# Delta rule: inverses of two successive pairs stated side by side, their transfers queued behind those stated last, and k times q a step behind q's convolution

## The chip, the core and the metric

The kernel runs on one core of a Trainium2 chip. The metric is the time of one execution on the device, in microseconds. A core has five engines that work at the same time, each through its own instructions in a fixed order: TensorE (PE in the profile; its weight loads are PEld), VectorE (DVE), ScalarE (ACT), GpSimd (POOL) and SyncE (SP). SP computes nothing here: it sends the transfers (DMAs) between device memory and on-chip memory, one after the other, and an instruction that waits for a semaphore holds up those behind it in its queue.

## What is computed

The program is one decoder layer in float32 on x of shape 4 x 512 x 512: a gated delta rule over 16 heads of 128, a cross attention, a self attention and a mixture of 8 experts. The change lies in the first part. Its reference, cut:

```
q = _causal_conv(x @ Wq.T, cw_q, cb_q)      # 4 taps, then silu; k and v the same
...
g = jnp.exp(-jnp.exp(A_log)[None, None, :] * jax.nn.softplus(a + dt_bias[None, None, :]))
beta = jax.nn.sigmoid(b)
q = _l2norm(q.reshape(Bb, Ss, H, DK))
k = _l2norm(k.reshape(Bb, Ss, H, DK))
...
def step(Sstate, inputs):
    q_t, k_t, v_t, g_t, beta_t = inputs
    retrieved = jnp.einsum('bhkv,bhk->bhv', Sstate, k_t)
    error = v_t - g_t[..., None] * retrieved
    update = k_t[..., :, None] * (beta_t[..., None] * error)[..., None, :]
    Snew = g_t[..., None, None] * Sstate + update
    o_t = jnp.einsum('bhkv,bhk->bhv', Snew, q_t)
    return (Snew, o_t)
...
o = o * jax.lax.rsqrt(jnp.mean(o * o, axis=-1, keepdims=True) + EPS) * norm_w
o = o * jax.nn.silu(x @ Wg.T)
return o @ Wo.T
```

## The kernel before

The 512 steps of the scan are taken in 4 chunks of 128. Within a chunk the steps become a linear system with a triangular matrix of 128 x 128, and its inverse makes them into matrix products. The work goes by **pairs**: pair m is two of the 16 heads of one sequence, 32 pairs in all (4 sequences of 8 pairs). A pair has four parts:

- stage1(m), lines 530 to 632: k's products (line 511), convolution (519, 522, 525), its turning round (554), its squared length ss (559, 565) and from it, on POOL, rk, ee, ke and nr (566 to 570; nr is appended to `factors`); the decays em (a scan on VectorE, 575, over the row that line 538 loads); the triangular matrices at (587), which go to device memory (588); then `load_blocks`, which loads their 32 diagonal blocks of 32 x 32, one a partition, as iA (642), and a table of identities as iT (641). After that q's convolution, qg = q times a row of decays (598, POOL; the row comes by another transfer of line 538), the product of k and q with its decays, pt (607, 609), and q's squared length, which goes through sr (616, 618) and a transfer (622) into rq, and is raised to a power on POOL (630, 631).
- stage2_inverse(m), lines 645 to 668: 31 elimination steps on the 32 blocks at once, each two instructions (654, 655) that depend on each other, on VectorE for even m and on POOL for odd m. Then the inverses and their transposes (659) go to device memory (658 into t_d, 660 into x_d) and come back as 128 x 128 tiles T (663) and X (665).
- stage2_values(m), lines 682 to 705: v's and the gate's products and convolutions (511 to 525), v turned round and scaled (694, 696); line 687 sends rq on its way to a row.
- stage3(m), lines 712 to 829: T and X are completed out of their 32-blocks (lines 726 to 760: four groups of small products, each waiting for a copy on ScalarE), rrow is loaded (764), and then come the chunks one after the other: r (778, 780), u (787, 789), the next state (797, 800 or 802) and the outputs (805, 807). At its end lines 819, 823, 827 and 828 scale the output and sum its squares. output(m), line 833, multiplies by Wo (852, 857).

The main loop (952 to 985) runs over m. In round m it takes the 15 steps of stage3(m), and after each of them one step of `rest`: `turns` gives every generator in it its number of steps, that is one of output(m-1), two of stage1(m+2), one of stage2_values(m+1) and two of inversions(m, ...). What is left of `rest` is stated after stage 3. This order of statement isn't yet the order in which the engines work: the layer below (a scheduler) orders each engine's instructions, by its own idea of what is ready when, and it keeps data dependences and the edges that `tc.issue_after(ins)` gives: whatever is stated inside that block for the engine of `ins` comes behind `ins` on that engine. The main loop so queues the rest behind the last of stage 3's vector instructions (`vital`), and the odd pairs' elimination steps behind the latest nr (`factors`). SP's transfers have no such edge.

`inversions` states the inverse of pair m+1 to its end, and only then, from step 10 of stage 3 on and if the blocks have been asked for, begins that of pair m+2, which is carried on in the next round (`begun`). `inverses` holds the blocks of a pair before its inverse, and T and X after it.

Weights are loaded ahead by line 502, the rows of decays by line 538, each into one buffer: the load waits until the last reader of what it overwrites is done. T has one buffer, X two.

Of the kernel before, what the change touches and what calls it, by code (L numbers as in the profile page):

```python
# [31 lines left out]
F32 = mybir.dt.float32  # L32
# [6 lines left out]
P = 128  # L39
B, S, D = 4, 512, 512  # L40
NT = B * S // P
TB = S // P
# [3 lines left out]
HG = 2  # L46
# [52 lines left out]
def decoder(ctx: ExitStack, tc: tile.TileContext, a: dict, out: bass.AP):  # L99
    nc = tc.nc  # L100
# [38 lines left out]
    def chain(*gs):  # L139
        for g in gs:  # L140
            yield from g
# [31 lines left out]
    def run(*gs):  # L173
        for g in gs:
            for _ in g:
                pass

    def turns(*gs):

        gs = [(g, n) for g, n in gs if g is not None]  # L180
        while gs:
            left = []
            for g, n in gs:
                if all(next(g, gs) is not gs for _ in range(n)):
                    left.append((g, n))
            gs = left
            yield
# [138 lines left out]
    with ExitStack() as st:  # L326
# [3 lines left out]
        w2 = st.enter_context(tc.tile_pool(name="a_2", bufs=2))  # L330
# [32 lines left out]
        inv_d = [[dram.tile([HG * TB, CH], F32, name=f"{k}_d{n}") for k in "tx"] for n in range(2)]  # L363
# [18 lines left out]
        def squares(d):  # L382

            return d[:, : P * P].rearrange("c (r t) -> r c t", r=P)

        def blocks(d):

            f = d.rearrange("c x -> (c x)").rearrange("(n x) -> n x", x=BLK)
            return f[:, : 32 * P].rearrange("n (r t) -> n r t", r=32)[:, :, 0:32]
# [4 lines left out]
        def scale(dst, src, by, p):  # L394

            for c in range(TB):
                nc.scalar.activation(dst[:, c, :], src[:, c, :], AF.Identity, scale=by[:, p * TB + c : p * TB + c + 1])

        seqs = {}

        def prologue(b):
# [128 lines left out]
        def stage1(m):  # L530
# [12 lines left out]
            for p in range(HG):  # L543
                t = live.tile([P, S], F32, name="kT")
# [6 lines left out]
            for p in range(HG):  # L551
# [3 lines left out]
                t = s1.tile([P, TB, P], F32, name="ktok")  # L555
# [22 lines left out]
            ats = []  # L578
# [15 lines left out]
            for p in range(HG):  # L594
                q = s1.tile([P, S], F32, name="qh")
                yield from conv(b, hg, p, 0, wq, q)
                g = live.tile([P, S], F32, name="qg", bufs=6)
                nc.gpsimd.tensor_tensor(g, q, mb[p], ALU.mult)
                qg.append(g)
                t = w2.tile([P, S], F32, name="cv", bufs=5)  # L600
                nc.scalar.activation(t, q, AF.Square)
                sq.append(t)
                yield
                pq = p_b.tile([P, TB, P], F32, name="pb")
                for c in range(TB):
                    cs = slice(c * P, (c + 1) * P)
                    nc.tensor.matmul(pq[:, c, :], kT[p][:, cs], q[:, cs], start=True, stop=True)
                t = live.tile([P, TB, P], F32, name="pt", bufs=6)
                nc.vector.tensor_tensor(t, pq, em[p], ALU.mult)
                pt.append(t)  # L610
                yield
# [13 lines left out]
            for p in range(HG):  # L625
                t = live.tile([P, TB, P], F32, name="kdec", bufs=4)
# [5 lines left out]
            keys[m] = (kT, kd_, qg, pt, nr, rq)  # L632


        inverses, begun, vital, factors = {}, {}, [], []

        def load_blocks(m, ats):

# [6 lines left out]
        def stage2_inverse(m):  # L645

            nb = HG * TB * 4
            A, T, W, ats = inverses.pop(m)
            eng = nc.vector if m % 2 == 0 else nc.gpsimd
            for i in range(31):  # L650
                n, w = 31 - i, i + 1
                u = W[:, : n * w].rearrange("p (a b) -> p a b", a=n)
                with tc.issue_after(factors[-1]) if m % 2 else ExitStack():
                    eng.tensor_tensor(u, A[:, i, i + 1 :].unsqueeze(2).to_broadcast([nb, n, w]), T[:, i, :w].unsqueeze(1).to_broadcast([nb, n, w]), ALU.mult)  # L654
                    eng.tensor_tensor(T[:, i + 1 :, :w], T[:, i + 1 :, :w], u, ALU.add)  # L655
                yield
            dT, dX = inv_d[m % 2]
            nc.sync.dma_start(blocks(dT), T)
            eng.tensor_copy(A, T.rearrange("p t j -> p j t"))
            nc.sync.dma_start(blocks(dX), A)  # L660
            yield
            t = w2.tile([P, HG * TB, P], F32, name="T", bufs=1)
            nc.sync.dma_start(t, squares(dT))
            x = w2.tile([P, HG * TB, P], F32, name="X", bufs=2)
            nc.sync.dma_start(x, squares(dX))
            Ts, Xs = ([v[:, p * TB : (p + 1) * TB, :] for p in range(HG)] for v in (t, x))
            inverses[m] = (Ts, Xs, ats)
            yield

        def inversions(m, step, turn):  # L670

            if m + 1 < NP:
                yield from begun.pop(m + 1) if m + 1 in begun else stage2_inverse(m + 1)
            if m + 2 < NP:
                while turn and (turn[0] < step or m + 2 not in inverses):
                    yield
                begun[m + 2] = stage2_inverse(m + 2)
                while turn:
                    next(begun[m + 2])
                    yield  # L680

        def stage2_values(m):

            b, hg = divmod(m, NHG)
            nr, rq = keys[m][4:]
            wv, wg = weights.pop((m, 2)), weights.pop((m, 3))
            nc.sync.dma_start(r_d[m % SLOTS].rearrange("c t -> (c t)").rearrange("(n k) -> n k", k=HG * TB), rq)
            v_, gs = [], []
            for p in range(HG):
                t = yield from conv(b, hg, p, 2, wv, None)  # L690
                yield
                tp = p_b.tile([P, TB, P], F32, name="pb")
                for c in range(TB):
                    nc.tensor.transpose(tp[:, c, :], t[:, c * P : (c + 1) * P], ident)
                v = w2.tile([P, TB, P], F32, name="vn", bufs=4)
                nc.vector.tensor_tensor(v, tp, along(nr[:, p * TB : (p + 1) * TB], P), ALU.mult)
                v_.append(v)
                yield
            load_weights(m + 1, 2)
            for p in range(HG):  # L700
                g = w2.tile([P, S], F32, name="gs", bufs=3)
                yield from conv(b, hg, p, 3, wg, g)
                gs.append(g)
            load_weights(m + 1, 3)
            pairs[m] = (v_, gs)
# [6 lines left out]
        def stage3(m):  # L712
# [1 line left out]
            b, hg = divmod(m, NHG)  # L714
            xnT, beta, gam, ngam, gend, gall = seqs[b]
            kT, kd_, qg, pt, _, _ = keys.pop(m)
            Ts, Xs, ats = inverses.pop(m)
            v_, gs = pairs.pop(m)

            half = [slice(p * 64, (p + 1) * 64) for p in range(HG)]  # L720
# [228 lines left out]

        run(itertools.islice(pair0, 3 * HG + 1))  # L950
        run(turns((stage2_inverse(0), 2), (chain(pair0, turns((stage1(1), 2), (stage2_values(0), 1))), 1), (prepare(), 1)))
        for m in range(NP):
            rest, turn = [], [0]
            if m == NP - 2:
                first.close()
                x_keep = top.enter_context(tc.tile_pool(name="x_keep", bufs=1, side="right", reuse_waits="tile"))
                wq, wpj = (x_keep.tile([P, KD, D], F32, name=n) for n in ("wq", "wpj"))
                nc.sync.dma_start(wq, a["b_wq"].rearrange("(k p) c -> p k c", p=P))
                nc.sync.dma_start(wpj, a["b_wp"].rearrange("(k p) c -> p k c", p=P))
                bq, bp = rows(x_keep, "bq", "b_bq", D), rows(x_keep, "bp", "b_bp", D)  # L960
                x_kT, x_val = x_keep.tile([P, KD, M], F32, name="x_kT"), x_keep.tile([P, 2, D], F32, name="x_val")
                nc.sync.dma_start(x_kT, x_kT_d)
                nc.sync.dma_start(x_val, x_val_d)
            if m == NP - 1:
                second.close()
                wx = top.enter_context(tc.tile_pool(name="b_x", bufs=2, side="right", reuse_waits="tile"))
                rest.append((cross(0), 2))
            if m:
                rest.append((chain(idle(1), output(m - 1)), 1))
            if m + 2 < NP:  # L970
                if (m + 2) % NHG == 0:
                    assert (m + 2) // NHG in seqs
                rest.append((stage1(m + 2), 2))
            if m + 1 < NP:
                rest.append((stage2_values(m + 1), 1))
                rest.append((inversions(m, 10, turn), 2))
            if (m + 4) % NHG == 0 and (m + 4) // NHG < B:
                rest.append((prologue((m + 4) // NHG), 1))
            rest = turns(*rest)
            for _ in stage3(m):  # L980
                with tc.issue_after(vital[-1]) if vital else ExitStack():
                    next(rest, None)
                turn[0] += 1
            turn.clear()
            run(rest)
        run(turns((output(NP - 1), 1), (cross(1), 2)))
# [573 lines left out]
```

## Time and profile before

| what | us |
|---|---|
| three runs | 4069.01, 4071.47, 4080.96 |
| median | 4071.47 |
| the profiled execution | 4070.2 |
| its span, from first to last instruction | 4068.4 |
| first product of stage 3 of pair 0 | 150.3 |
| the same of pair 31 | 2310.8 |

From 150 to 2311 us the core works on the delta rule, and after that on the parts that the change doesn't touch. Between the first products of stage 3 of two successive pairs lie 66 to 76 us: mostly some 67 where the later pair is odd, some 73 where it is even.

The views used are: the page (busy time and shares of each engine), the list of waits (who waited for whom: us in total, times, longest us), the timeline of one engine (start, duration, engine, line, operation, what it writes and reads, and in brackets the idle time before it and what ended it), and the windows (busy time, granted clock, share of the DMA engines and GB/s in a stretch). SPq is SP's queue; a transfer's line there tells when it was sent, not when it landed. A line of matmuls counts two records for each float32 product.

### The profile page before, as it was taken

The page shows a single profiled execution, that of the slowest core. Times are in us where ns is not written, and L with a number is a line of the kernel's source. Part 1 is how long each engine was busy: PE and PEld are TensorE (multiplying, and loading weights), DVE is VectorE, ACT ScalarE, POOL GpSimd, SP SyncE. Part 2 cuts the span into 40 slices and gives each one's busy share as a digit, 9 for nine tenths or more (in the row PEclk, how much of TensorE's full clock was granted, in tenths as well). Part 3 has the DMA queues.
Part 4 walks back from the last instruction along what each step waited for, and adds up shares of the span by engine and source line. Part 5 has one row for each costly group of instructions (what it writes and reads, how often), then busy time and mean ns, then how long its engine had stood idle before and what let it go on. Part 6 is the DMA issues. An engine that isn't in the chain of part 4 may idle for free. (4 is left out here: it accounts for less than half of the span.)

```text
span 4068.4 us, 48733 instructions
## 1 busy us (share of the span) xinstructions
PE 3452.6 (85%) x16466; PEld 1942.1 (48%) x16466; DVE 2273.2 (56%) x4923; ACT 1572.8 (39%) x4379; POOL 1390.2 (34%) x1941
## 2 busy tenths in 40 slices
PE   5878787877978787887878788999999999899797
PEld 3545444444544444444444444555555555555343
DVE  5556656565755656665565545555665666555211
ACT  2434443333534343443334324444444444444121
POOL 1435434443543444354344522121211211211342
PEclk8989998898989898998989878999999999999898
DMA  5332333323333322323232334544444544456344
GB/s 152 88 103 90 103 90 103 94 74 103 101 98 86 113 82 85 107 87 118 85 102 68 96 118 134 163 148 145 149 140 139 162 141 143 130 170 221 74 83 92
DMA packets 391880, 465.56 MB, mean 114 GB/s; under 512 B 128451, under 2 KB 242115, under 8 KB 391440
## 3 DMA queue, kind: packets, MB, share of 16 engines
q1 hardware_dynamic: 380080, 438.03, 35.2%
q0 software_dynamic: 10112, 21.58, 2.9%
q10 hardware_dynamic: 1440, 2.84, 0.2%
q8 instruction: 132, 2.16, 0.2%
q14 instruction: 116, 0.95, 0.1%
HBM read 401.76 MB, written 64.81 MB: 115 GB/s over the span
## 5 line engine op out<-in xcount | busy, mean ns | idle before, releaser
L511 PE MATMUL pb<-xnT,w 128*128 128x512 f32 x2048 | 1027.7, 641 | 0.0
L522 DVE SCALAR_TENSOR_TENSOR cv<-pb,pp,cv 128x509 f32<-128x509 f32 (+2 forms) x576 | 423.3, 742 | 481.7 <-ACT cv L519 475.0
L511 PEld LDWEIGHTS pb<-xnT,w 128*128 128x128 f32 x2048 | 398.5, 207 | 423.8 <-issue 397.5
L1102 PE MATMUL pb<-c_q,hT 128*128 128x512 f32 x768 | 360.9, 609 | 6.3 <-DMA c_q<-in_c_wq_dram 3.7
L654 POOL TENSOR_TENSOR iW<-iA,iT 32x31 f32<-32x31 f32 (+15 forms) x496 | 259.3, 523 | 154.6 <-issue 69.5
L655 POOL TENSOR_TENSOR iT<-iT,iW 32x31 f32<-32x31 f32 (+15 forms) x496 | 285.8, 576 | 38.9
L726 PE MATMUL pb<-T,at 128*32 128x32 f32 x512 | 19.8, 236 | 325.2 <-DMA T<-t_d 325.2
L566 POOL TENSOR_TENSOR rk<-ss,mhalf 128x8 f32<-128x8 f32 x32 | 52.7, 1648 | 665.7 <-DVE ss L565 665.7
L519 ACT ACTIVATE cv<-pb,pp 128x512 f32<-128x512 f32 x192 | 148.7, 775 | 321.3 <-PE pb L511 321.1
L852 PE MATMUL pb<-wot,og 128*128 128x512 f32 x512 | 250.2, 611 | 4.7 <-DVE cv L522 4.7
L1208 PE MATMUL pw<-c_o,oT 128*128 128x512 f32 x512 | 241.3, 602 | 2.9 <-DVE oT L1200 2.9
L655 DVE TENSOR_TENSOR iT<-iT,iW 32x31 f32<-32x31 f32 (+15 forms) x496 | 229.9, 464 | 11.5
L1102 PEld LDWEIGHTS pb<-c_q,hT 128*128 128x128 f32 x768 | 144.0, 196 | 163.3 <-issue 152.6
L654 DVE TENSOR_TENSOR iW<-iA,iT 32x31 f32<-32x31 f32 (+15 forms) x496 | 215.2, 434 | 9.2
L1174 ACT ACTIVATE e<-pb,nm,rq 128x128 f32<-128x128 f32 (+3 forms) x256 | 157.0, 618 | 139.4 <-DVE nm L1172 105.8
L274 POOL TENSOR_SCALAR x_e<-x_e 128x1024 f32<-128x1024 f32 x64 | 68.0, 1063 | 334.1 <-ACT x_e L269 246.9
L1198 PE MATMUL po<-eT,val 128*128 128x512 f32 x320 | 169.8, 623 | 7.2 <-ACT eT L1196 4.4
L726 PEld LDWEIGHTS pb<-T,at 128*32 128x32 f32 x512 | 15.7, 146 | 331.7 <-DMA T<-t_d 328.8
L1168 PE MATMUL pb<-kT,qT 128*128 128x256 f32 (+3 forms) x576 | 162.7, 409 | 0.8 <-ACT x_e L269 0.8
L269 ACT ACTIVATE x_e<-pb,nm 128x256 f32<-128x256 f32 x256 | 118.3, 477 | 103.0 <-DVE nm L266 103.0
L1465 PE MATMUL pb<-w_gu,eT 128*128 x312 | 142.2, 599 | 3.5 <-issue 3.5
L1030 POOL TENSOR_TENSOR rope_s<-q,tab 128x128 f32<-128x128 f32 x64 | 35.2, 551 | 321.0 <-DVE q L1132 281.6
(330 smaller groups left out, 6622.3 us busy)
## 6 DMA issues: line engine op xcount, KB each, us to landing
c_o<-in_c_wo_dram SPq DMA_DIRECT2D x128, 512.0 KB, 4.3
c_q<-in_c_wq_dram SPq DMA_DIRECT2D x128, 512.0 KB, 4.7
w<-in_a_w_dram SPq DMA_DIRECT2D x124, 512.0 KB, 4.2
row<-g_d SPq DMA_DIRECT2D x64, 512.0 KB, 4.1
at_d<-at SPq DMA_DIRECT2D x64, 256.0 KB, 2.2
T<-t_d SPq DMA_DIRECT2D x32, 512.0 KB, 4.2
X<-x_d SPq DMA_DIRECT2D x32, 512.0 KB, 6.0
rrow<-r_d SPq DMA_DIRECT2D x32, 512.0 KB, 3.8
```

The source lines that it names most:

```text
L511: nc.tensor.matmul(pj, wt[:, kd, p * P : (p + 1) * P], xnT[:, kd, :], start=kd == 0, stop=kd == KD - 1)
L519: nc.scalar.activation(ac, pj, AF.Identity, bias=cb[:, m, h : h + 1], scale=cw[:, m, h, 3:4])
L522: nc.vector.scalar_tensor_tensor(ac[:, j:], pj[:, : S - j], cw[:, m, h, 3 - j : 4 - j], ac[:, j:], ALU.mult, ALU.add)
L654: eng.tensor_tensor(u, A[:, i, i + 1 :].unsqueeze(2).to_broadcast([nb, n, w]), T[:, i, :w].unsqueeze(1).to_broadcast([nb, n, w]), ALU.mult)
L655: eng.tensor_tensor(T[:, i + 1 :, :w], T[:, i + 1 :, :w], u, ALU.add)
L852: nc.tensor.matmul(pw, og[p][:, c * P : (c + 1) * P], wot[:, p, :], start=p == 0, stop=p == HG - 1)
L1102: nc.tensor.matmul(pj, hT[:, kd, :], w[:, kd % 2, :], start=kd == 0, stop=kd == KD - 1)
L1168: nc.tensor.matmul(ps[:, m, k * P : (k + w) * P], qT[g][:, n + m, :], kT[:, g, j : j + w, :], start=True, stop=True)
L1174: nc.scalar.activation(e[n + m][:, :nk], ps[:, m, :nk], AF.Exp, bias=nm[:, n + m : n + m + 1], scale=rq, accum_out=es[:, n + m : n + m + 1])
L1198: nc.tensor.matmul(po, val[:, g, :], eT, start=k == 0, stop=k == c)
L1208: nc.tensor.matmul(pw, oT[:, h + m, :], w[:, m, :], start=g == 0 and h + m == 0, stop=g == 3 and h + m == 3)
L1465: nc.tensor.matmul(pg, hT[:, kd, :], w_gu[:, bass.ds(e, 1), kd, :, :], start=kd == 0, stop=kd == KD - 1)
```

## The change

The inverses of m+1 and m+2 advance by one step each in turn, and that of m+2 begins as soon as its blocks have been asked for; that of pair 1 is begun before the loop. Finished inverses have a dictionary of their own (`joined`), so that `m + 2 in inverses` means that blocks wait. The two transfers to device memory, and the two back, are stated inside `issue_after` of whatever instruction of SP was stated last. In stage1 one more `yield` stands between q's square and the product of k and q, so that this product and all of stage1 that follows are stated a step later. No operation is added or taken away.

```diff
@@ -396,6 +396,10 @@
+        def behind(engine):
+
+            return tc.issue_after(next(i for i in reversed(nc.cur_bb.bb.instructions) if i.engine == engine))
+
@@ -601,6 +605,7 @@
                 nc.scalar.activation(t, q, AF.Square)
                 sq.append(t)
                 yield
+                yield
                 pq = p_b.tile([P, TB, P], F32, name="pb")
@@ -632,7 +637,7 @@
-        inverses, begun, vital, factors = {}, {}, [], []
+        inverses, begun, joined, vital, factors = {}, {}, {}, [], []
@@ -653,31 +658,35 @@
-                yield
+                yield i
             dT, dX = inv_d[m % 2]
-            nc.sync.dma_start(blocks(dT), T)
-            eng.tensor_copy(A, T.rearrange("p t j -> p j t"))
-            nc.sync.dma_start(blocks(dX), A)
-            yield
+
+            with behind(mybir.EngineType.SP):
+                nc.sync.dma_start(blocks(dT), T)
+                eng.tensor_copy(A, T.rearrange("p t j -> p j t"))
+                nc.sync.dma_start(blocks(dX), A)
+            yield 31
             t = w2.tile([P, HG * TB, P], F32, name="T", bufs=1)
-            nc.sync.dma_start(t, squares(dT))
             x = w2.tile([P, HG * TB, P], F32, name="X", bufs=2)
-            nc.sync.dma_start(x, squares(dX))
+            with behind(mybir.EngineType.SP):
+                nc.sync.dma_start(t, squares(dT))
+                nc.sync.dma_start(x, squares(dX))
             Ts, Xs = ([v[:, p * TB : (p + 1) * TB, :] for p in range(HG)] for v in (t, x))
-            inverses[m] = (Ts, Xs, ats)
-            yield
-
-        def inversions(m, step, turn):
-
-            if m + 1 < NP:
-                yield from begun.pop(m + 1) if m + 1 in begun else stage2_inverse(m + 1)
-            if m + 2 < NP:
-                while turn and (turn[0] < step or m + 2 not in inverses):
-                    yield
-                begun[m + 2] = stage2_inverse(m + 2)
-                while turn:
-                    next(begun[m + 2])
-                    yield
+            joined[m] = (Ts, Xs, ats)
+            yield 32
+
+        def inversions(m, turn):
+
+
+            open_ = True
+            while open_ or turn:
+                if open_:
+                    open_ = next(begun[m + 1], None) is not None
+                if turn and m + 2 in inverses:
+                    begun.setdefault(m + 2, stage2_inverse(m + 2))
+                    next(begun[m + 2], None)
+                yield
+            begun.setdefault(m + 2, stage2_inverse(m + 2))
@@ -714,7 +723,7 @@
-            Ts, Xs, ats = inverses.pop(m)
+            Ts, Xs, ats = joined.pop(m)
@@ -949,6 +958,7 @@
+        begun[1] = stage2_inverse(1)
         for m in range(NP):
@@ -973,14 +983,13 @@
-                rest.append((inversions(m, 10, turn), 2))
+                rest.append((inversions(m, turn), 2))
...
-                turn[0] += 1
             turn.clear()
```

More of the change, by code (lines that the diff above doesn't have):

```diff
@@ L655, in stage2_inverse @@
                     eng.tensor_tensor(T[:, i + 1 :, :w], T[:, i + 1 :, :w], u, ALU.add)
-                yield
[L657 to L660, printed above, removed]
-            yield
-            t = w2.tile([P, HG * TB, P], F32, name="T", bufs=1)
-            nc.sync.dma_start(t, squares(dT))
-            x = w2.tile([P, HG * TB, P], F32, name="X", bufs=2)
-            nc.sync.dma_start(x, squares(dX))
-            Ts, Xs = ([v[:, p * TB : (p + 1) * TB, :] for p in range(HG)] for v in (t, x))
-            inverses[m] = (Ts, Xs, ats)
-            yield
-        def inversions(m, step, turn):
-            if m + 1 < NP:
-                yield from begun.pop(m + 1) if m + 1 in begun else stage2_inverse(m + 1)
-            if m + 2 < NP:
-                while turn and (turn[0] < step or m + 2 not in inverses):
-                    yield
-                begun[m + 2] = stage2_inverse(m + 2)
-                while turn:
-                    next(begun[m + 2])
-                    yield
+                yield i
+            dT, dX = inv_d[m % 2]
+            with behind(mybir.EngineType.SP):
[3 more added lines that the diff above has]
+            yield 31
+            t = w2.tile([P, HG * TB, P], F32, name="T", bufs=1)
+            x = w2.tile([P, HG * TB, P], F32, name="X", bufs=2)
+            with behind(mybir.EngineType.SP):
+                nc.sync.dma_start(t, squares(dT))
+                nc.sync.dma_start(x, squares(dX))
+            Ts, Xs = ([v[:, p * TB : (p + 1) * TB, :] for p in range(HG)] for v in (t, x))
+            joined[m] = (Ts, Xs, ats)
[8 more added lines that the diff above has]
+                    next(begun[m + 2], None)
+                yield
+            begun.setdefault(m + 2, stage2_inverse(m + 2))
         def stage2_values(m):
```

## The prediction

> **What bounds the kernel now.** The page comes first. TensorE is the busiest engine, but its share is a mean over different stages:
>
> ```profile
> PE 3452.6 (85%) x16466; PEld 1942.1 (48%) x16466; DVE 2273.2 (56%) x4923; ACT 1572.8 (39%) x4379; POOL 1390.2 (34%) x1941
> ```
>
> The page's chain is no help here (it ends in a transfer at once), so the list of waits is next:
>
> ```profile
> POOL rk L566 <- DVE ss L565: 665.7, 32, 33.9
> ...
> PE pb L726 <- DMA T<-t_d: 325.2, 29, 15.1
> ...
> PE pb L607 <- ACT qh L525: 55.6, 18, 5.3
> ```
>
> TensorE loses 325 us at line 726, the first product of stage 3, for the block inverse T to land; line 607 (k times q) loses 56 us. The reader sees that the delta rule's 2,200 us run at the pace of a loop: inverse, transfers, stage 3. Pass m is here the time from the start of stage 3 of pair m-1 to that of pair m (round m-1 of the loop); odd and even passes differ, so I read the timeline of each.
>
> Pass 11 (odd: the inverse runs on POOL), SP's queue, then POOL, then TensorE:
>
> ```profile
> 890.65 0.32 SPq L642 DMA_DIRECT2D iA<-at_d  x1
> 914.79 0.32 SPq L658 DMA_DIRECT2D t_d<-iT  x1
> 916.80 0.30 SPq L660 DMA_DIRECT2D x_d<-iA  x1
> 917.20 0.51 SPq L663 DMA_DIRECT2D T<-t_d  x1
> ...
> 920.20 0.83 SPq L538 DMA_DIRECT2D row<-g_d  x1
> 921.45 1.15 SPq L622 DMA_DIRECT2D rq<-sr  x2
> 922.66 0.57 SPq L538 DMA_DIRECT2D row<-g_d  x1
> 923.33 0.38 SPq L502 DMA_DIRECT2D w<-in_a_w_dram  x1
> ```
>
> ```profile
> 914.49 0.28 POOL L655 TENSOR_TENSOR iT<-iT,iW 32x31 f32<-32x31 f32 x1
> 914.83 1.94 POOL L659 COPY iA<-iT 32x1024 f32<-32x1024 f32 x1
> 916.85 2.60 POOL L598 TENSOR_TENSOR qg<-qh,row 128x512 f32<-128x512 f32 x2
> ```
>
> ```profile
> 921.86 0.26 PE L726 MATMUL pb<-T,at 128*32 128x32 f32 x1 [10.43 <-DMA T<-t_d]
> ```
>
> POOL's last step ends at 914.77; SP, which stood 24 us at t_d, sends at once; T lands 7 us later and TensorE, idle since 911.4, starts. POOL itself is late because its queue stands at rk (line 566) until 881.94, 27 us into the pass, and 21 of the 31 steps are behind it.
>
> Pass 10 (even: on DVE) ends otherwise; DVE, then SP:
>
> ```profile
> 844.93 1.27 DVE L823 TENSOR_TENSOR cv<-po,rrow 128x512 f32<-128x512 f32 x2
> 846.13 0.17 DVE L654 TENSOR_TENSOR iW<-iA,iT 32x31 f32<-32x31 f32 x1
> 846.33 0.18 DVE L655 TENSOR_TENSOR iT<-iT,iW 32x31 f32<-32x31 f32 x1
> ```
>
> ```profile
> 846.23 0.32 SPq L764 DMA_DIRECT2D rrow<-r_d  x1
> 846.64 0.38 SPq L658 DMA_DIRECT2D t_d<-iT  x1
> 848.55 0.32 SPq L660 DMA_DIRECT2D x_d<-iA  x1
> 850.81 0.38 SPq L663 DMA_DIRECT2D T<-t_d  x1
> ```
>
> The last step stands behind lines 819 and 823, which wait for TensorE's end (842.99), and t_d behind rrow: it takes 4.2 us to land where t_d's median is 2.6. T lands at 855.0, 12 us after TensorE went idle. Over all passes the idle time before line 726 is 10 us in plain odd passes, 12 in even ones, nearly 0 in passes 5, 13 and 21.
>
> [...] nothing left SP from 890.97 to 914.79. So a queue's order is a dependence. [...] Here the granted clock is 0.50 from 918 to 926, and line 511's next twelve records take 7.63 us, against 0.43 each later (5.2). So a wait of 8 or 18 us costs the same restart as one of 12[...]. [...] DVE's step of 192 elements took 1.22 us beside POOL's line 598, and 0.35 us alone (835.24).
>
> **The change, part by part.** I compared the order of the built programs, engine by engine. No instruction is added or removed; only places change.
>
> *Two inverses side by side.* Every step is stated earlier, but the built order moves by only one step: on POOL 11 steps (before: 10) stand ahead of the next rk and 20 (21) behind it. This saves one step, 0.58+0.63 us and gaps, 1.3 us per odd pass. rk still waits for ss, since that is TensorE's and ACT's doing. On DVE, 12 (14) of an even inverse's instructions stand behind the last r of its pass (line 780), and all of them now stand ahead of 819 and 823 in the plain passes. From the second r: one step less and 2.6 us of 819/823 out of the way, against 0.6 us for line 609, which now stands behind r: the steps end 6.1 us after r (0.28 a step, 1.13 a scan of line 575, 0.61, 0.28, 1.13, and 2.65 for the last ten) instead of 8.4 (838.12 to 846.51). In odd passes the first DVE step now stands ahead of r of chunk 2 and waits for iA; r and what follows it would be late. iA is issued at 890.65 and POOL's own first step came 3.4 us after its iA, so r goes from 892.85 to about 894: 1 us of TensorE's work, hidden by the 10 us at line 726.
>
> *Transfers behind those stated last.* This decides. On SP before, odd pass: iA, t_d, x_d, T, w, X, iT, row, rq, row, w. Now: iA, w, row, row, rq, w, t_d, x_d, T, r_d, X, rrow, iT. The first row transfer overwrites the row that line 598 reads, so it waits for POOL's second line 598 — which stands behind the inverse's last step and line 659. So t_d, free at 914.77, has to wait for 0.06+1.94+0.08+2.60 = 4.7 us on POOL and then for SP to send row 0.83, row 0.57, rq 1.15, w 0.38 and gaps 0.3 = 3.2 us. Ahead of it in the DMA engines are then three transfers of 512 KB (524,288 bytes). By the view of windows such packets moved at 354 to 391 GB/s at 924 to 928 us, 1.4 us each, 4.3 in all: about 1 us more than the 3.2 that sending takes. This last is the unknown: from 0 to 3 us (T, w and X, sent within 1.9 us at 917.2, had X land at 925.4). Sum: 4.7+3.2+1.0-1.3 = +7.6 us per plain odd pass, on a path where TensorE is already idle, so nothing hides it. X moves behind r_d, which waits for rq's power on POOL; it still lands some 3 us after T, and line 736 needs it 8 us after. rq leaves 6.1 us after the inverse's end, before 6.7, so POOL's lines 630 and 631 behind it are not late. The transfers that move ahead of t_d were waited for by no TensorE instruction, so they gain nothing.
>
> Odd passes: six plain at 7.6 = 45.6; passes 1 and 3, without the saved step, 8.9 each = 17.8; pass 29, with one row, 6.5; passes 9, 17, 25, where t_d already had a part of this queue, 6 each = 18; passes 5, 13, 21, where g_d's two transfers (line 489, behind TensorE's 483 at 1063.1) now also stand ahead of t_d: that gives T at about 1074 instead of 1064.7, 9.4 each = 28.2. Sum +116.
>
> Even passes: t_d leaves 2.3 us earlier after r, r itself is about 0.5 us earlier (line 778 now ahead of 607), and rrow is no longer ahead (1.6), but row and w are, partly landed (+0.8): -3.6. Bounds: 0 and -5.5. Twelve such = -43. In passes 4, 12, 20 rrow stays ahead; [...] -2.5 each = -7.5. TensorE still idles some 8 us there, so the restart stays.
>
> *k times q a step later.* In TensorE's order the first 607 of a pass keeps its place behind 778, where it waits 3.2 us for qh in even passes; line 511 only moves from before line 694 to after it. The second 607 goes behind 778, which is the 0.5 us counted. The 56 us stay: 0, at best -10.
>
> Sum: 116-50.5 = +65 us. The profiled execution took 4070.2 (span 4068.4, 1.8 around it); with +65, 4135. The median shown, 4071.5, is 1.3 above that execution, inside its runs.
>
> **Rivals.** (1) The transfers ahead of t_d cost more: if they land at the pace seen for X, each odd pass loses 3 us more, and even passes gain only 1.5: 161-23 = +138, 4208. For it: t_d's 128-byte packets are slow beside others. Against: 4.2 us is the worst seen. (2) Even passes gain what odd ones lose: within 12 us of before, 4070; it needs -7 us per even pass, more than the chain r, steps, t_d, T allows by its durations. (3) Faster: the place is line 726 in even passes. [...] the 12 us wait and the 2.4 us restart would go, 15 times: -14 each, -210, against +116: 3976; a milder form gives 4050. It decides from -8 us per even pass. Against it: t_d and T alone need 2.6+4.2 us after the last step. (4) The built order does not show on the chip: 4070.
>
> **How the numbers follow.** The forecast (+35 to +110) has 0.63; rival 1 0.22; 2 and 4 together 0.07; 3 0.08. Predicted 4135, range 4078 to 4195: it takes in the unknown cost on both sides and the upper half of (2). 0.3% is 12 us, about what a measurement of this kernel can tell: slower 0.86, same 0.06, faster 0.08.
>
> **What would show it.** Idle before line 726: near 18 us in plain odd passes, 8 in even ones, 9 in passes 5, 13, 21. SP's wait of 24 us moves from line 658 to 538 (on POOL line 598). POOL's rk wait and line 607's stay. Wrong, if T of an odd pair lands under 10 us after POOL's last step.

## The result, and the profile after

| | before | changed | |
|---|---|---|---|
| median of the runs, us | 4073.22 | 4166.65 | 1.0228 times, 95% interval 1.021 to 1.0245 |
| span of the profiled execution, us | 4068.4 | 4165.4 | +97.0 |
| from stage 3 of pair 0 to that of pair 31, us | 2160.4 | 2259.2 | +98.8 |
| the 15 odd passes 1 to 29, us | 1017.9 | 1150.1 | +132.2 |
| the 15 even passes 2 to 30, us | 1105.9 | 1072.7 | -33.2 |

The change makes the kernel 2.3% slower, and all of it lies in the delta rule: odd passes lose, even ones gain less. The last three rows are worked out from the starts of the first product of stage 3. Pass 31 (36.6 us before, 36.4 after) is in neither of the last two; it and pass 1 (62.8 us before) lie outside the 66 to 76 us given above. In the changed kernel lines lie 4 to 9 further down: 598 is now 602, 607 is 612, 654 and 655 are 659 and 660, 658 is 665, 663 is 672, 726 is 735, 780 is 789, 819 and 823 are 828 and 832. In the kernels of the experiments they differ by a few lines again; the tile names in each line tell what it is.

The list of waits of the changed kernel (us in total, times, longest us), engines first, then SP's own:

```profile
POOL rk L570 <- DVE ss L569: 793.4, 32, 30.8
PE pb L735 <- DMA T<-t_d: 363.5, 30, 21.1
...
PE pb L612 <- ACT qh L529: 52.7, 17, 4.4
```

```profile
SPq L542 <- POOL qg L602: 330.4, 31, 19.4
```

SP's list before had these two instead:

```profile
SPq L658 <- POOL iT L655: 335.2, 15, 24.0
SPq L538 <- POOL qg L598: 87.0, 16, 5.8
```

TensorE waits for T 38 us longer than before (325.2). That is less than the 97 us lost, because its own work in the plain odd passes ends 4.8 us later too (61.1 against 56.3 us into the pass, table of the experiments). SP's wait at t_d for POOL's last step is gone from its list; instead the one at the row transfer, for qg on POOL, has grown from 87.0 to 330.4 us. The wait at k times q (55.6 before) is where it was, and that for ss at rk, which was to stay, has grown from 665.7 to 793.4.

Pass 11 of the changed kernel, the timelines of SP, POOL and TensorE (start, duration). The pass runs from 886.10 to 961.09:

```profile
934.83 0.34 SPq L506 DMA_DIRECT2D w<-in_a_w_dram  x1
949.75 0.80 SPq L542 DMA_DIRECT2D row<-g_d  x2
950.66 1.11 SPq L627 DMA_DIRECT2D rq<-sr  x2
951.82 0.58 SPq L506 DMA_DIRECT2D w<-in_a_w_dram  x1
952.77 0.33 SPq L665 DMA_DIRECT2D t_d<-iT  x1
953.15 0.55 SPq L667 DMA_DIRECT2D x_d<-iA  x1
957.27 0.38 SPq L672 DMA_DIRECT2D T<-t_d  x1
```

```profile
944.82 0.24 POOL L660 TENSOR_TENSOR iT<-iT,iW 32x31 f32<-32x31 f32 x1
945.12 1.97 POOL L666 COPY iA<-iT 32x1024 f32<-32x1024 f32 x1
947.17 2.56 POOL L602 TENSOR_TENSOR qg<-qh,row 128x512 f32<-128x512 f32 x2
```

```profile
961.09 0.26 PE L735 MATMUL pb<-T,at 128*32 128x32 f32 x1 [14.08 <-DMA T<-t_d]
```

POOL's last step ends at 945.06, but SP stands at the row until both qg are done (949.73), sends row, rq and w, and comes to t_d at 952.77: 7.7 us late. t_d is followed by T 4.5 us later, where it was 2.4 in pass 11 before. T's producer, the inverse, is no later in its pass than before (59.3 us in the mean of the plain odd passes, 59.6 before); the place of its transfer in SP's queue is.

Pass 10, even, SP and TensorE:

```profile
876.48 0.58 SPq L506 DMA_DIRECT2D w<-in_a_w_dram  x1
877.15 0.38 SPq L665 DMA_DIRECT2D t_d<-iT  x1
878.07 0.32 SPq L667 DMA_DIRECT2D x_d<-iA  x1
882.21 0.38 SPq L672 DMA_DIRECT2D T<-t_d  x1
```

```profile
886.10 0.26 PE L735 MATMUL pb<-T,at 128*32 128x32 f32 x1 [9.13 <-DMA T<-t_d]
```

Here t_d leaves at once after VectorE's last step (877.00), which no longer stands behind lines 828 and 832. But two rows, rq and w went out in the six microseconds before it (from 871.21 on), and T follows 5.1 us behind t_d. So the idle time falls from 12 to 9 us, no further.

### The profile page after: what moved, and what is told of

Its sections match the earlier page's. It is cut to its first block, busy times and chain, and to the rows that moved or that the text cites. A ratio compares the mean times of both kernels' runs of the same rounds, so it can differ in the third digit from the quotient of the medians.

```text
span 4165.4 us, 48807 instructions
## 1 busy us (share of the span) xinstructions
PE 3476.8 (83%) x16466; PEld 1971.9 (47%) x16466; DVE 2267.8 (54%) x4923; ACT 1578.9 (38%) x4379; POOL 1390.3 (33%) x1941
## 5 line engine op out<-in xcount | busy, mean ns | idle before, releaser
L515 PE MATMUL pb<-xnT,w 128*128 128x512 f32 x2048 | 1017.9, 638 | 0.0
L570 POOL TENSOR_TENSOR rk<-ss,mhalf 128x8 f32<-128x8 f32 x32 | 52.7, 1648 | 793.4 <-DVE ss L569 793.4
L659 DVE TENSOR_TENSOR iW<-iA,iT 32x31 f32<-32x31 f32 (+15 forms) x496 | 230.0, 464 | 18.2 <-DMA iA<-at_d 9.1
L660 DVE TENSOR_TENSOR iT<-iT,iW 32x31 f32<-32x31 f32 (+15 forms) x496 | 212.3, 428 | 10.7
```

Source lines behind the costliest of these rows:

```text
L515: nc.tensor.matmul(pj, wt[:, kd, p * P : (p + 1) * P], xnT[:, kd, :], start=kd == 0, stop=kd == KD - 1)
```

## The experiments

The table gives, worked out from the timelines, means over the passes that the prediction calls plain, the six odd ones (7, 11, 15, 19, 23, 27) and the twelve even ones (2, 6, 8, 10, 14, 16, 18, 22, 24, 26, 28, 30), in us from the pass's start: the inverse's end, t_d sent, T sent, TensorE's end, and the pass's length (TensorE's start on T).

| kernel | odd: inverse | t_d | T | TensorE | pass | even: inverse | t_d | T | TensorE | pass |
|---|---|---|---|---|---|---|---|---|---|---|
| before | 59.6 | 59.7 | 62.3 | 56.3 | 66.6 | 64.7 | 64.9 | 69.2 | 61.3 | 73.3 |
| changed | 59.3 | 66.7 | 71.7 | 61.1 | 75.6 | 62.0 | 62.0 | 66.7 | 61.9 | 70.6 |
| e1 steps and yield | 58.7 | 58.8 | 61.2 | 60.8 | 65.5 | 61.5 | 61.6 | 64.2 | 61.5 | 68.8 |
| e2 queueing alone | 59.8 | 71.4 | 75.6 | 56.5 | 79.6 | 65.0 | 65.1 | 69.5 | 61.6 | 73.6 |
| e3 yield alone | 60.1 | 60.1 | 62.7 | 57.9 | 67.1 | 62.1 | 62.2 | 66.1 | 61.6 | 70.0 |
| e12 steps alone | 59.2 | 59.2 | 61.7 | 60.1 | 66.3 | 62.5 | 63.1 | 67.4 | 61.7 | 71.3 |
| e4 queueing in even only | 59.0 | 59.1 | 61.5 | 61.3 | 65.9 | 61.7 | 61.8 | 66.2 | 61.7 | 70.1 |
| e5 row by POOL | 59.1 | 61.2 | 66.2 | 61.5 | 70.5 | 62.1 | 62.2 | 66.8 | 62.2 | 70.7 |
| e6 late first step | 59.2 | 66.7 | 71.8 | 58.2 | 75.6 | 61.6 | 61.7 | 66.3 | 61.5 | 70.2 |
| e7 no yield | 59.5 | 71.4 | 75.7 | 60.4 | 79.7 | 61.9 | 62.7 | 66.9 | 61.1 | 70.8 |
| e8 POOL ahead | 46.8 | 46.8 | 49.3 | 57.9 | 57.8 | 64.8 | 68.9 | 72.8 | 61.4 | 77.0 |
| e9 ahead, behind qg, 10 | 53.2 | 53.2 | 55.7 | 65.8 | 65.7 | 61.6 | 61.6 | 64.2 | 60.7 | 68.8 |
| e10 the same, 7 | 62.1 | 62.1 | 66.1 | 66.3 | 70.0 | 61.8 | 61.8 | 64.4 | 60.9 | 69.0 |
| e11 ahead, behind rq | 46.8 | 46.8 | 49.3 | 57.6 | 57.5 | 59.2 | 59.4 | 62.5 | 59.8 | 66.9 |

The theory: the queue order on SP makes the loss (Q). The rivals: the side-by-side steps, which make r wait for iA (S), and the k times q step (K).

**e1: the changed kernel without the queueing.** At both places:

```diff
-            with behind(mybir.EngineType.SP):
+            with ExitStack():
```

> The changed kernel with the four transfers of the inverse stated plainly (not queued behind SP's last); side-by-side steps and the k times q step kept. Theory Q (the queue order on SP makes the loss): in odd passes t_d leaves at the inverse's end again, T about 2.5 us later, so odd passes return to 66 to 68 us (from 75.6), while even passes keep most of their gain (-2.5 to -3 us in the plain ones): 4030 to 4055 us. Rival S (the side-by-side steps make it: VectorE's first even step waits for iA ahead of r and TensorE ends 3 to 6 us later in odd passes): the odd passes stay at 70 to 75, 4110 to 4160. Rival K (the k times q step makes it): about 4160.

Measured 4018.49 us, ratio to before 0.9853 (0.983 to 0.9875). The sign turns: without the queueing the change is 1.5% faster than the kernel before. S and K fall. SP in pass 11 of e1 (905.9 is the pass's end):

```profile
899.08 0.32 SPq L665 DMA_DIRECT2D t_d<-iT  x1
901.07 0.30 SPq L667 DMA_DIRECT2D x_d<-iA  x1
901.49 0.50 SPq L672 DMA_DIRECT2D T<-t_d  x1
```

t_d stands at the head of SP's queue, waiting; T follows 2.4 us behind it. It came out better than expected mainly because even passes gained more too (68.8 against 70.6 with the queueing).

**e2: the kernel before with the queueing alone.** The same two `with behind(...)` blocks put around the transfers of the kernel before.

> The kernel before with only the queueing of the four transfers behind those stated last. Q: odd passes as in the changed kernel (+7.5 to +9 us each, about +120 to +130 in all), even passes no shorter than before, since their steps still stand behind lines 819 and 823 and t_d stands behind w and rrow (0 to +1.5 each): 4190 to 4215 us, slower than the whole change. S and K: 4073 within 12.

Measured 4257.0, ratio 1.044 (1.0418 to 1.0463): Q's direction, but twice the loss of the whole change, and above the range expected. Pass 11 of e2, SP and then POOL:

```profile
979.82 0.32 SPq L542 DMA_DIRECT2D row<-g_d  x1
980.23 1.11 SPq L626 DMA_DIRECT2D rq<-sr  x2
981.39 0.58 SPq L542 DMA_DIRECT2D row<-g_d  x1
985.76 0.33 SPq L693 DMA_DIRECT2D r_d<-rq  x1
986.18 0.38 SPq L506 DMA_DIRECT2D w<-in_a_w_dram  x1
986.61 0.42 SPq L663 DMA_DIRECT2D t_d<-iT  x1
```

```profile
983.75 0.24 POOL L634 TENSOR_SCALAR rq<-rq 128x8 f32<-128x8 f32 x1 [3.95 <-DMA rq<-sr]
984.07 1.67 POOL L635 TENSOR_TENSOR rq<-rq,mhalf 128x8 f32<-128x8 f32 x1
```

A second wait: r_d, now also ahead of t_d, needs rq's power on POOL, which needs rq to land. In the mean of the plain odd passes t_d leaves 11.7 us after the inverse's end.

**e3: the kernel before with the second yield alone, and e12: with the side-by-side steps alone** (e1 without the yield). For e3:

```diff
                 sq.append(t)
                 yield
+                yield
```

> The kernel before with only the second yield (k times q a step behind the convolution of q). In the built order this alone takes lines 819 and 823 from ahead of the even inverse's last steps and rrow from ahead of t_d. Q: odd passes as before within 1 us; plain even passes -2 to -3 us, 12 of them: 4040 to 4060 us. K: 4120 or more. If the even gain comes from the side-by-side steps alone: 4073 within 8.

> The kernel before with the side-by-side steps alone (no queueing, no second yield). Lines 819 and 823 stand behind the even inverse's last steps here too, one step less behind the last r, but r_d and w stand ahead of t_d in even passes. By the prediction's even term, -50 less what r_d costs, and TensorE's later end in odd passes hidden by the wait for T: 4025 to 4055 us. If the side-by-side steps help only together with the yield (which took 56 us together with them and 26 alone): 4055 to 4085.

e3: 4049.05, ratio 0.9934 (0.9909 to 0.9959). e12: 4041.2, ratio 0.9917 (0.9901 to 0.9933). Each gains by itself, in even passes (70.0 and 71.3 against 73.3), and together 58 us (e1). Either takes lines 819 and 823 from ahead of VectorE's last step: the inverse ends 2.6 or 2.2 us earlier. They differ in what stands ahead of t_d on SP: e12 keeps r_d there, and t_d leaves 0.6 us after the inverse's end, in e3 0.1.

**e4: queueing for even inverses only.**

```diff
-            with behind(mybir.EngineType.SP):
+            with behind(mybir.EngineType.SP) if m % 2 == 0 else ExitStack():
```

> The changed kernel with the queueing for even inverses only (odd ones state their transfers plainly). Q: odd passes 66 to 68 us, even passes as in the changed kernel (70.4): 4035 to 4055 us, within 12 of the version with no queueing at all, that is, the queueing brings nothing in even passes either. S: 4110 to 4160.

Measured 4031.76, ratio 0.9899 (0.9875 to 0.9923). The odd passes are back (65.9), so their queueing is the loss. In even ones the queueing costs some 13 us against e1, a little over the 12 expected: with w just ahead of it t_d is followed by T 4.4 us later, without it 2.6 us later (e1).

**e5: the row's load on POOL's own queue.** Which of the two costs the odd passes, the wait or the bytes?

```diff
-                nc.sync.dma_start(chunks(t), g_d[b, n, ...])
+                (nc.gpsimd if n else nc.sync).dma_start(chunks(t), g_d[b, n, ...])
```

> The changed kernel with the load of row1 (the one that waits for POOL's second line 602) put on POOL's own DMA queue, behind that line; everything else on SP stays behind-queued. Ahead of an odd t_d stand then only row0, rq (free when ScalarE's sr is there, 58.8 us into the pass) and w. Theory W (most of the odd loss is the wait of SP at row for POOL): t_d leaves some 1.5 to 2 us after the inverse's end instead of 7.7, odd passes lose 5 to 6 us of their 75.6, 15 of them: 4075 to 4100 us. Rival D (the load is the bytes ahead of t_d in the DMA engines, which stay about the same): odd passes lose 2 us at most, 4135 or more.

Measured 4086.22, ratio 1.0015 (1.0006 to 1.0025), against 4167.13 for e6 beside it, which has the changed kernel's time: some 80 us of the loss are gone with one transfer on another queue. T still follows t_d by 5.0 us, as in the changed kernel (5.0), so that part of the loss stays. The row's issue takes 0.64 us on POOL, and what is gone is SP's wait at the row for qg (330.4 us in the changed kernel, the longest 19.4). Pass 11 of e5, POOL and then SP:

```profile
919.99 0.64 POOL L542 DMA_DIRECT2D row<-g_d  x1 [0.30 <-DMA w<-in_a_w_dram]
```

```profile
914.77 1.11 SPq L627 DMA_DIRECT2D rq<-sr  x2
916.04 0.47 SPq L506 DMA_DIRECT2D w<-in_a_w_dram  x1
916.55 0.43 SPq L665 DMA_DIRECT2D t_d<-iT  x1
```

The row goes out from POOL after t_d and holds nobody up. t_d leaves 2.1 us after the inverse's end in the mean, behind the other row, rq and w, none of which waits for POOL. Passes 5, 13 and 21 keep their 78.3 us: there g_d's own transfers stand ahead of t_d.

**e6: the changed kernel with the first even step stated later**, so that it stands behind both r of chunk 2.

```diff
-            open_ = True
+            open_, wait = True, 4 * (m % 2 == 0)
...
-                if turn and m + 2 in inverses:
+                if turn and m + 2 in inverses and wait:
+                    wait -= 1
+                elif turn and m + 2 in inverses:
```

> The changed kernel with the first step of an even inverse stated two turns later, so that it stands behind both r of chunk 2 on VectorE in odd passes (nothing else moves past the last r). If T bounds the odd passes (theory Q), TensorE ends about 3 us earlier there and idles as much longer: 4166 within 12. If the wait for iA ahead of r costs time in itself (S): 12 x 3 to 15 x 4 us less, 4105 to 4130.

Measured 4167.13, ratio 1.0203 (1.0186 to 1.022), the changed kernel's time. TensorE ends 2.9 us earlier in odd passes (58.2), and they are as long (75.6). VectorE in pass 11 of the changed kernel shows what was taken away:

```profile
925.23 0.74 DVE L659 TENSOR_TENSOR iW<-iA,iT 32x31 f32<-32x31 f32 x1 [0.66 <-DMA iA<-at_d]
925.90 0.33 DVE L789 SCALAR_TENSOR_TENSOR r<-ps,ngam,vn 128x128 f32<-128x128 f32 x1
```

So a delay of 3 us in TensorE's work is hidden, as long as T comes later still.

**e7: the changed kernel without the second yield** (e3's line taken out).

> The changed kernel without the second yield. In SP's built order r_d, which waits for rq to land and for POOL's power (line 631), then stands ahead of an odd t_d, as in the version with the queueing alone, where t_d left 11.5 us after the inverse's end and not 7.7. If that is the reason why the queueing alone lost more than the whole change, odd passes lose about 4 us more each, 15 of them: 4210 to 4235 us. If the yield is worth the same wherever it stands (27 us, as on the kernel before): 4185 to 4200. By the prediction's term for k times q (0 to 10 us): 4160 to 4176.

Measured 4223.32, ratio 1.0347 (1.033 to 1.0364): r_d stands ahead of an odd t_d again, 11.9 us after the inverse's end as in e2 (11.7). So the yield's share in the whole change is 50 to 57 us (the spans differ by 4216.2 - 4165.4, the medians by 4223.32 - 4166.65), and most of it came through SP's queue: the odd passes are 43 us longer in sum than in the changed kernel, the even ones 6.

**e8: more of POOL's steps ahead of rk.** e1 shows that T bounds the plain odd passes still (TensorE idles 4.7 us). POOL meanwhile stands at rk. So e1, with e6's late step, and:

```diff
+            extra = 7 * ((m + 1) % 2)
             while open_ or turn:
...
+                if open_ and extra:
+                    extra -= 1
+                    next(begun[m + 1])
```

> The version without queueing, with the late first step of e6, and with seven more of an odd inverse's steps stated early, so that 18 and not 11 stand ahead of the next rk on POOL, which idles there for some 20 us. The odd inverse ends 7 x 1.35 = 9 us earlier (near 50 us into the pass) and T lands near 57, when TensorE ends at about 57: plain odd passes 58 to 60 us instead of 66, passes 5, 13, 21 by TensorE 67 to 69 instead of 70.5: 3910 to 3950 us. If steps ahead of rk make rk late, or VectorE's steps bind in their place: 3970 to 4020.

Measured 4014.03, ratio 0.9826 (0.981 to 0.9843): a miss, inside the range of the alternative. The odd inverse ends 12 us earlier and TensorE never idles in odd passes (57.8), but plain even passes went from 68.8 to 77.0. Pass 10 of e8 (from 767.90), POOL and then SP:

```profile
833.03 1.26 POOL L602 TENSOR_TENSOR qg<-qh,row 128x512 f32<-128x512 f32 x1
```

```profile
814.29 0.34 SPq L506 DMA_DIRECT2D w<-in_a_w_dram  x1
834.32 0.80 SPq L542 DMA_DIRECT2D row<-g_d  x2
835.21 1.11 SPq L627 DMA_DIRECT2D rq<-sr  x2
836.37 0.58 SPq L665 DMA_DIRECT2D t_d<-iT  x1
```

The steps were placed ahead of the even pass's second qg, for which SP's row waits 20 us, and the even t_d stands behind it: the mechanism of the odd passes again, one pass earlier. This explains 4.1 us (t_d leaves at 68.9, the inverse ends at 64.8). Another 3.3 us are the inverse itself, which ended at 61.5 in e1: while POOL works on its moved steps, VectorE's last steps take longer than in e1 (one of 60 elements 0.74 us, against 0.21). In pass 10, e8 first, then e1:

```profile
828.68 0.74 DVE L659 TENSOR_TENSOR iW<-iA,iT 32x60 f32<-32x60 f32 x1
```

```profile
830.65 0.21 DVE L659 TENSOR_TENSOR iW<-iA,iT 32x60 f32<-32x60 f32 x1
```

What makes them longer there no run shows.

**e9 and e10: POOL's steps kept behind the latest qg**, with ten and seven steps stated early.

```diff
-                nc.gpsimd.tensor_tensor(g, q, mb[p], ALU.mult)
+                factors.append(nc.gpsimd.tensor_tensor(g, q, mb[p], ALU.mult).ins)
```

> e8 with ten instead of seven steps stated early, and POOL's steps queued behind the latest qg (line 602) as well as behind the latest factors, so that none of the moved steps stands ahead of the second qg of an even pass, for which SP's row waits. Theory: in e8 the seven steps did stand ahead of it, SP stood at row until 66.4 us into an even pass and t_d left 5 us after VectorE's last step; so the 113 us that odd passes gained went back in even ones. With this, odd passes stay at 57 to 60 us (TensorE never idle there) and even ones go back to 68 to 71: 3900 to 3940 us. If even passes are long because the shorter odd pass leaves VectorE too few steps done: they stay at 73 or more and the time is 3960 to 4010.

> e9 with seven steps. In its built order row and w stand ahead of an odd t_d on SP again, but row's producer, the second qg, stands ahead of the inverse's last step on POOL, so that the wait is over before t_d is ready: odd passes 57 to 61 us, even 68 to 71, 3905 to 3950 us. If a row ahead of t_d costs by itself, whatever its producer's place: odd passes 63 or more, above 3970.

e9: 4016.92, ratio 0.9858 (0.9841 to 0.9874); e10: 4081.0, ratio 1.0018 (1.0011 to 1.0025). Both missed. In e9 plain even passes are back (68.8), as the theory had it, but the steps now stand ahead of rq's power, so that r_d is late and X behind it; TensorE then waits inside stage 3 (pass 11 of e9):

```profile
833.98 0.26 PE L741 MATMUL pb<-T,at 128*32 128x32 f32 x1 [7.73 <-DMA T<-t_d]
847.54 0.43 PE L751 MATMUL pb<-Y,X 128*64 128x32 f32 x4 [5.74 <-DMA X<-x_d]
```

e10 has this wait too (61.5 us in all, 62.2 in e9): in pass 11 of either, r_d leaves only some 9 us into the pass, X behind it, and rk starts at 34.6 us in the mean of the plain odd passes, where it was 27.3 in e1. Passes 4, 12 and 20, which the table leaves out, show the same wait for rq on SP: r_d there stands ahead of the even t_d (with rrow between them), which leaves 8.5 us after VectorE's last step (0.3 in e1), and TensorE idles 28 us (13 to 15 in e1). In e10, besides, the odd inverse's last step stands behind qg, and waits with it:

```profile
915.23 1.97 POOL L602 TENSOR_TENSOR qg<-qh,row 128x512 f32<-128x512 f32 x1 [4.06 <-issue]
917.29 0.23 POOL L659 TENSOR_TENSOR iW<-iA,iT 32x31 f32<-32x31 f32 x1
```

**e11: the steps behind rq's power instead**, seven stated early:

```diff
-            nc.gpsimd.tensor_tensor(rq, rq, mhalf[:, 0 : HG * TB], ALU.pow)
+            factors.append(nc.gpsimd.tensor_tensor(rq, rq, mhalf[:, 0 : HG * TB], ALU.pow).ins)
```

> The version without queueing, with the late first step and seven more steps stated early as in e8, but POOL's steps that are stated after line 636 (rq's power) are queued behind it, so that the moved steps fill the time between rq's power and the next rk, where POOL idles, and stand ahead of neither the qg that SP's row waits for (e8) nor the power that SP's r_d waits for (e9). POOL then has 17 steps of some 1.4 us, 23 us, from about 67 us into an even pass, done before rk can start 27 us into the odd one. Theory: odd passes 57 to 60 us, where TensorE bounds them, even ones 68 to 71: 3900 to 3950 us. If even passes lengthen whatever the order, because VectorE has less time in a shorter odd pass: 3970 to 4010.

Measured 3885.72, ratio 0.9545 (0.9527 to 0.9564): 4.5% faster than the kernel before, below the range expected, since the even passes became shorter too (66.9 against 68.8 in e1; VectorE's inverse ends 2.3 us earlier, which was not traced further). POOL from pass 10 into pass 11 (which starts at 796.3):

```profile
792.56 1.67 POOL L636 TENSOR_TENSOR rq<-rq,mhalf 128x8 f32<-128x8 f32 x1
794.30 0.28 POOL L659 TENSOR_TENSOR iW<-iA,iT 32x60 f32<-32x60 f32 x1
...
817.41 0.67 POOL L660 TENSOR_TENSOR iT<-iT,iW 32x252 f32<-32x252 f32 x1
823.42 1.65 POOL L570 TENSOR_TENSOR rk<-ss,mhalf 128x8 f32<-128x8 f32 x1 [5.34 <-DVE ss L569]
```

```profile
POOL rk L570 <- DVE ss L569: 350.6, 31, 20.2
...
PE pb L741 <- DMA T<-t_d: 128.8, 16, 14.1
```

17 steps fill the time in which POOL stood at rk and are done 5.3 us before rk can start. TensorE's wait for T falls from 325 to 129 us, nearly all of it now in even passes, and plain odd passes last as long as TensorE's work (57.5).

## Why the prediction was right, and where it was off

The forecast (+65, 4135, slower) named the mechanism and the place, and both stand. The size was short by a third: odd passes lost 16 us more than reckoned and even ones gained 17 less, two errors that add up. In the plain odd passes T is sent 12.4 us after POOL's last step and lands later still, where a landing under 10 us would have proved it wrong. The cause is the row's wait for qg on POOL, with t_d behind it, in odd passes: e1, e4 and e5 show it by taking it away. Its steps, one by one:

- **The sum of a plain odd pass**, +7.6 predicted, +9.0 measured. The POOL wait and SP's sending (4.7 + 3.2) measured 7.4. The backlog (what stands ahead of t_d in the DMA engines), put at 1.0 with a bound of 3, was the term mis-sized: T followed t_d 2.4 us later than before, 0.4 of which came back as a quicker landing of T. The traces' packet records show where the 2.4 us lie: t_d's first packet of 128 bytes starts 2.80 us after t_d is sent, before it was 0.85. They take 13 to 14 ns each in both kernels; packets of 4,096 bytes (159 ns, the median), those of the rows and w, fill the time until then. So the store waits for what is ahead of it and is not slower itself. And of the 1.3 us of the saved elimination step 0.3 came: rk itself started 1.0 us later (27.8 against 26.8 us into the pass, means of the six). About half of this is there without the queueing (27.3 in e1); what delayed rk was not tried.
- **The other odd passes**: 5, 13, 21 +10.8 each (9.4 predicted), 9, 17, 25 +7.4 (6), 1 and 3 +7.1 (8.9), 29 +9.0 (6.5). All odd passes +132 for +116.
- **Even passes**, -50.5 predicted, -33.2 measured. The inverse ended 2.7 us earlier, as reckoned (2.8). The term that failed is the next: rrow's leaving from ahead of t_d was counted as -0.8 net of row and w, and it brought 0.0. e1 shows why: with t_d ahead of w the pass is 1.8 us shorter still. In passes 4, 12 and 20 the -2.5, an estimate, were -0.3.
- **k times q: "0, at best -10"** is the step that was wrong, though the sum hardly shows it. The wait at line 607 stayed, as said, but the yield alone is worth -27 us (e3), and -50 to -57 within the change (e7), since it moves what is stated behind it in stage1: lines 819 and 823 on VectorE, r_d on SP. The built order of the whole change already held these moves, so they were in the sum, but under the name of the side-by-side steps.
- **r's wait for iA** was priced at 1 us and measures 2.9 (e6). It was rightly called hidden, and it is most of the reason why the idle time before line 735 is 14.5 us in plain odd passes, not the 18 foretold: TensorE ends 4.8 us later than before, of which 1.9 stay in e6, nearly what the yield alone brings (1.6 in e3).
- **Rival 3**, even passes short enough for the clock's restart to go, didn't come about: the idle time there stayed near 9 us. In passes 1 to 29 of the changed kernel the waits before line 735 are 7.9 to 21.1 us, each is followed by a granted clock of 0.50, and line 515's first twelve records take 6.6 to 8.1 us, whatever the wait (7.51 in pass 11, where the clock is 0.50 from 961 to 964 us). So a wait of 8 us did cost the restart that one of 18 does. How short a wait must be for the restart to stay away was not shown; it is absent after pass 5 of the kernel before, where TensorE waited 1.2 us: twelve records take 5.42 us, at a granted clock of 1.00 from 496 to 502 us. In e11's odd passes TensorE doesn't wait: after pass 11 line 515's first ten records take 4.56 us, against 6.65 in the changed kernel.

In sum, the queueing costs 180 us alone (e2) and some 150 beside the other two parts (from 0.9853 to 1.0228), which by themselves gain 58.

## What to carry to other kernels

Putting a transfer "behind what was stated last" on an in-order queue made it wait here for everything that those ahead of it waited for (t_d left 7.4 us after the inverse's end in plain odd passes, in e2 11.7), so look up each one's semaphore before you choose its place: a load into a single buffer waits for that buffer's last reader (SP at the row for qg: 330.4 us in all), and the reader may stand behind the very work whose result you want to send. Where such a load must be, let the engine that frees its buffer send it (e5: 4086 us, against 4167). When work is moved into an idle gap of an engine, name what each instruction that it passes feeds: three placements of such steps, each of which held up something that SP waits for, gave 4014, 4017 and 4081 us, and the fourth, between rq's power and rk, 3886.

## What the runs showed of the hardware

A store of 128 KB (t_d, 32 partitions of 4 KB) was followed by the load that depends on it 2.4 to 2.6 us later when nothing large had left just ahead of it. When a row, rrow or w of 512 KB each had, it took 3.9 to 5.1 us (means of the table's passes; 3.1 in e11's even ones). In even passes of e4 and e1 the two kernels differ in the queueing alone, and the times are 4.4 and 2.6. I had expected 1 us more. The store's packets of 128 bytes took 13 to 14 ns each in either case (the median one of 4,096 bytes took 159, so 0.04 ns a byte against 0.10); it was their start that came later.

The row's issue from POOL held POOL for 0.64 us (e5), a small price beside the wait that it took off SP. And a VectorE step of 60 elements on 32 partitions took 0.74 us while POOL worked on steps of its own (e8), and 0.21 us in e1, as in the kernel before with POOL idle (843.47 us).
